# A third buffer for the sums of slots 4 and 12 in the last three groups of a pairwise-bias attention loop, on one Trainium2 core

## The chip, the cores and the metric

The kernel runs on one NeuronCore of a Trainium2 chip. The metric is device time in microseconds, the median of three runs. One further execution was taken by the hardware profiler; durations, waits and the chain of work come from that one.

## The reference, cut to what matters

Two layers work on x of shape 2 x 512 x 32 x 32. Layer 0 is a deformable attention with a learned position bias, followed by an MLP; layer 1 is a plain attention over the 1024 positions. The bias of layer 0 is the part around the change: for each of 16 (batch, head) groups, every one of the 1024 query positions is paired with 64 sampled key positions, and each pair goes through a small network with a hidden width of 128.

```
bias = sign(pos) * log1p(abs(pos))           # pos: 1024 queries x 64 keys x 2
bias = relu(bias @ cpb_w1 + cpb_b1)          # 2 -> 128
bias = relu(bias @ cpb_w2 + cpb_b2)          # 128 -> 128
bias = bias @ cpb_w3 + cpb_b3                # 128 -> 1
sim  = q k^T + bias;  attn = softmax(sim);  out = attn v
x    = x + out_w out + out_b                 # the projection
x    = x + mlp_w2 gelu(mlp_w1 bn(x) + b1) + b2
# layer 1: q, k, v = x W^T + b;  x = x + (softmax(q k^T / sqrt(512)) v) Wp^T + bp
```

## The kernel before

**The loop over slots.** Each of the 16 groups is cut into 16 slots of 4 keys (`NSL = 16`), so the main loop runs over 256 slots, `s = 0..255`. For each slot:

- `st_layer1` (L678) makes the first hidden layer `h` of slot `s + 2` on DVE from two tables `ta` and `tb`. `h` has three buffers.
- `st_layer2` (L695) multiplies `h` by the 128 x 128 weight in four parts z = 0..3 of 32 output channels each. A part is 16 matmuls into one PSUM tile `ps` of 128 x 1024; the pool `zp` has three such tiles. The trace shows every fp32 matmul as two records, so a slot is 64 records. ScalarE (ACT) empties each part with a ReLU: z = 0 and 2 into `rx` (L705), z = 1 into a sums tile, z = 3 into `ub` (both L707).
- `st_sum` (L715) adds z = 0 to z = 1 and z = 2 to z = 3 on DVE.
- An accumulating DMA, issued from POOL (L717), adds `ub` to the slot's sums tile. Further DMAs then fold and join the sums of neighbouring slots: `add` (L734, accumulating, POOL queue) and `move` (L741, plain, SP queue), each chained behind the one before it. The list `due` says at which slot each is issued.
- `st_tables` (L658, L666) makes `ta` and `tb` on ACT for the next four slots once every four slots. It is held behind the eviction of z = 1 of the slot that calls it (`tc.issue_after(evicted[s][0])`).

`st_layer3` (L825) then contracts a whole group's folded sums on the TensorE into `sim`, 22 slots after the group's first slot for the last three groups and 27 slots after it for the others. Softmax (`softmax_steps`) runs in small pieces inside later slots; its transposes on the TensorE are `pt` (L842) and `pb` (L877), and `sim` starts with the product of L806.

**Sums tiles.** Which sums tile a slot's z = 1 part goes to depends on `s % 8`:

```
name, bufs = (
    ("rx", 3), (("u8", 4), ("uo", 3), ("uc", 2), ("uo", 3), ("u4", 2), ("uo", 3), ("uc", 2), ("uo", 3))[s % 8],
    ("rx", 3), ("ub", 3),
)[z]
o = lp.tile([P, 2, 512], F32, name=name, bufs=bufs)
```

In the trace `u8` and `u4` both appear as `u`. Slots with `s % 8 == 4` are the group's slots 4 and 12; they go to `u4`, which has two buffers. For groups before the last three (`s < FULL = 208`) slot 4's sums are joined into slot 0's by the last level of DMAs, and `st_layer3` reads two tiles of a group. In the last three groups this level is left out, and `st_layer3` reads four: those of slots 0, 4, 8 and 12 (in the last group the tiles of its last four slots singly, in place of that of slot 12 alone). So a `u4` tile then lives until its group's `st_layer3`.

**What sets the order.** A scheduler orders each engine's instructions when the program is built, from the program's order, from hints such as `issue_after` and from when buffers come free. At run time each engine works through its own list in order.

**Behind the loop.** The projection of batch 0 is a Strassen-like product of 7 parts (`project`, L1024). It needs sums of its operands beside the operands: `op_blocks` lays them out, `spread` (L125, L128) makes sums of `qa`, `fold` (L119) sums of `vp`. For batch 0, three sums of `qa` are in `op0x` and one overwrites a block of `qa`; the eight operations are put on DVE one at a time in the loop, four slots apart, from the slot `ready` on at which the preparation of the last keys ends. These tiles are in the pool `op`, which is opened at that slot. The order of the parts is 1, 2, 5, 6, 7, 3, 4; the sum number 3 of `spread`, `x[6]`, is read by the last of them alone.

The MLP follows in 8 units (two batches, four parts). `layer1` of a unit makes three interleaved pairs of products in `twice` (L160, with evictions at L166, L170, L172 and L176), writes them to seven blocks `hm[:, 0..6]`, applies GELU (L1096) and makes the sums for `layer2` (L1077), for which blocks 4, 5 and 6 are overwritten at the end. In the first unit the remaining product of `c11` is made first (`first`, L1136 to L1137), copied to `r3`, which is `hm[:, 5]`, added to `c11` at step 13.5 and followed by the GELU at step 19.5. Step 14 starts the third pair of products, whose results go to `hm[:, 4]` and `hm[:, 5]`.

Of the kernel before, what the change touches and what calls it, by code (L numbers as in the profile page):

```python
# [8 lines left out]
F32 = mybir.dt.float32  # L9
# [5 lines left out]
P = 128  # L15
# [42 lines left out]
def conv_seq_kernel(ctx: ExitStack, tc: tile.TileContext, x, xt, kst, pst, cst, vec, wsm, outw, w1, w2, wl, wlt, brow, out):  # L58
    nc = tc.nc
# [56 lines left out]
    def fold(engine, w, sign=ALU.add, which=range(4)):  # L116
        for i in which:
            o, u, v = FOLD[i]
            engine.tensor_tensor(w[o], w[u], w[v], ALU.add if i % 2 else sign)  # L119

    def spread(x, which=range(4)):
        for i in which:
            if i % 2 == 0:
                o, u = ((4, 0), (1, 3))[i // 2]
                nc.vector.tensor_tensor(x[o], x[u], x[1], ALU.subtract)  # L125
            else:
                o, u, v = ((5, 4, 3), (6, 5, 2))[i // 2]
                nc.vector.scalar_tensor_tensor(x[o], x[u], -1.0, x[v], ALU.mult, ALU.subtract)  # L128
# [7 lines left out]
    def plus(out, a, b_, op=ALU.add):  # L136
        nc.vector.tensor_tensor(out, a, b_, op)  # L137
# [53 lines left out]
    def op_blocks(b, parts, wsum):  # L191
        v, q = vp[:, b * NCH : b * NCH + NCH, :], qa[:, b]
        w = [v[:, k : k + 2, n : n + 256] for k, n in ((0, 0), (2, 0), (2, 256), (0, 256))]
        x = [q[:, k : k + 2, n : n + 512] for k in (0, 2) for n in (0, 512)]
        return w + [wsum[:, j] for j in range(3)], x + [parts[:, j] for j in range(3)]

    zp = ctx.enter_context(tc.tile_pool(name="zp", bufs=3, space=PSUM))
    simpp = tc.tile_pool(name="simp", bufs=2, space=PSUM)
# [8 lines left out]
    with tc.tile_pool(name="lp", bufs=2) as lp:  # L207
# [350 lines left out]
        def later():  # L558

            for c in range(NCH):  # L560
                ps = flat("psu")
                for f_, h_, f, h in QUADS:
                    nc.tensor.matmul(
                        ps[h_, f * 512 : f * 512 + 256], wv[f_, c * P + 64 * f : c * P + 64 * f + 64],
                        ow_s[f_, c, h * 256 : (h + 1) * 256], start=True, stop=True,
                    )
                for f_, h_, f, h in QUADS:
                    nc.scalar.copy(uo[f_, c, h * 256 : (h + 1) * 256], ps[h_, f * 512 : f * 512 + 256])
                if c % 2 == 1:
                    yield  # L570
            yield from sample(0)
            for ci in range(1, len(CHAINS)):
                yield from chain(ci)
                yield from sample(ci)
# [113 lines left out]
        def st_layer2(s):  # L688
            h1 = h1s.pop(s)
            r = []  # L690
            for z in range(4):
                ps = zp.tile([P, 2, 512], F32, name="ps2")
                for h in range(2):
                    for q in range(4):
                        nc.tensor.matmul(  # L695
                            ps[32 * q : 32 * q + 32, h, :], cw2[:, 32 * z : 32 * z + 32],
                            h1[:, 16 * h : 16 * h + 16, q, :], start=True, stop=True,
                        )
                name, bufs = (
                    ("rx", 3), (("u8", 4), ("uo", 3), ("uc", 2), ("uo", 3), ("u4", 2), ("uo", 3), ("uc", 2), ("uo", 3))[s % 8],  # L700
                    ("rx", 3), ("ub", 3),
                )[z]
                o = lp.tile([P, 2, 512], F32, name=name, bufs=bufs)
                if z % 2 == 0:
                    nc.scalar.activation(o, ps, AF.Relu, bias=sc[:, 4 + z : 5 + z])  # L705
                else:
                    nc.scalar.activation(o, ps, AF.Relu, bias=sc[:, 4 + z : 5 + z], scale=sc[:, z : z + 1])  # L707
                r.append(o)
                if z % 2 == 1:
                    evicted.setdefault(s, []).append(nc.cur_bb.bb.instructions[-1])  # L710
            sums[s] = r
# [69 lines left out]
        FULL = NS - 3 * NSL  # L781
# [103 lines left out]
        bg = later()  # L885
# [4 lines left out]
        for s in range(NS):  # L890
            if s > 0:
                st_sum(s - 1, 2)
            for _, go, a in sorted(due.get(s, ()), key=lambda e: e[0]):
                go(a)
            if s % 4 == 0 and s // 4 + 1 < 4 * NG:
                load_tables(s // 4 + 1)
            if s + 2 < NS:
                st_layer1(s + 2)
            st_layer2(s)


            if s % 4 == 0 and s // 4 + 1 < 4 * NG:
                with tc.issue_after(evicted[s][0]):
                    st_tables(s // 4 + 1)
            st_sum(s, 0)

            if bg is not None and (s % 4 or s < 124):
                with tc.issue_after(evicted[s][1]):
                    next(bg, None)
            if bg is not None and state.get(len(CHAINS) - 1, 0) is None:  # L910

                bg = None
                php.__exit__(None, None, None)
                opp = tc.tile_pool(name="op", bufs=1, side="right")
                op = opp.__enter__()
                op0 = op_blocks(
                    0, op.tile([P, 3, 2, 512], F32, name="op0x"), op.tile([P, 3, 2, 256], F32, name="op0w")
                )
                ready = s
            if bg is None and s > ready and (s - ready) % 4 == 0 and (s - ready) // 4 <= 8:  # L920
                i = (s - ready) // 4 - 1
                if i < 4:
                    spread(op0[1], (i,))
                else:
                    fold(nc.vector, op0[0], which=(i - 4,))

            if tails and (s % (2 if s < 60 else 4) or s >= NS - NSL):
                with tc.issue_after(evicted[s][s % 4 == 0]):
                    if next(tails[0], 0) is not None:
                        tails.pop(0)  # L930
            for t in (27, 22):
                if s % NSL == t % NSL and s >= t and (s - t < FULL) == (t == 27):
                    st_layer3(s - t)
                    tails.append(softmax_steps((s - t) // NSL))
# [4 lines left out]
                pass  # L939
        tail = softmax_steps(NG - 1)  # L940
        next(tail)


    def load_g(g, i):
# [27 lines left out]
    with ExitStack() as top, tc.tile_pool(name="wp", bufs=1) as wp:  # L972
# [120 lines left out]
        def layer1(p, we, w, xb, xe, hm, others=(), early=False):  # L1093
            def gelu(blk, src, scale=1.0):
                for m in range(2):
                    nc.scalar.activation(  # L1096
                        hm[:, blk, m, :], src[:, m, :], AF.Gelu,
                        bias=col("mb1", 4 * p + 2 * (blk // 2) + m), scale=scale,
                    )

            c11, c12, c21, c22, r5, r3 = (hm[:, j] for j in range(6))

            def weights(q, j):
                a = FIRST_W[PARTS[q][0]]
                return [inner_w(w, we, a, a - 1)[j]]

            def moving(q, j):
                b_ = FIRST_X[PARTS[q][1]]
                return [inner_x(xb, xe, b_, b_ - 1)[j]]

            def dest(g, m, h):
                return hm[:, 2 * g : 2 * g + 2, m, 256 * h : 256 * h + 256]

            def done(g):
                if g == 0:
                    plus(c12, c12, c11)
                elif g == 1:
                    plus(c22, c22, c12)
                    plus(c21, c21, c22)
                    gelu(2, c21, -1.0)  # L1120
                else:
                    plus(c22, c22, r5)
                    gelu(3, c22, -1.0)
                    plus(c12, c12, r5)
                    plus(c12, c12, r3)
                    gelu(1, c12)

            def second():
                ps = mq.tile([P, 2, 512], F32, tag="ps2", name="sw")
                product(w, xb)(ps, 0, 0)  # L1130
                plus(c11, c11, ps)
                gelu(0, c11)

            def first():
                ps = mq.tile([P, 2, 512], F32, tag="ps2", name="sw")
                product(w, xb)(ps, 0, 0)  # L1136
                nc.scalar.copy(r3, ps)  # L1137

            plain = ((21, second),)
            if early:  # L1140
                plain = (-1, first), (13.5, lambda: plus(c11, c11, r3)), (19.5, lambda: gelu(0, c11))
            twice(mq, ((1, 6), (4, 7), (5, 3)), weights, moving, dest, done, (*plain, *others))
            spread([hm[:, j] for j in range(7)])

# [52 lines left out]
        for i, (b, p) in enumerate(units):  # L1197

            j, k = divmod(i, NCH)
# [8 lines left out]
            hm = cp.tile([P, 7, 2, 512], F32, tag="big", name="hm")  # L1208
# [388 lines left out]
```

## Time and profile before

| | |
|---|---|
| median of 3 runs | 2617.9 us (2617.56 to 2618.49) |
| the profiled execution | 2619.14 us, its span 2617.3 us |
| PE busy | 2599.8 us (99% of the span) |
| DVE busy | 2301.5 us (88%) |
| ACT busy | 1752.4 us (67%) |
| POOL busy | 980.2 us (37%) |
| L695, second layer | 16384 records, 1773.3 us |
| L678, first layer on DVE | 257 instructions, 1131.6 us, 4404 ns each |

The span is the time from the first to the last instruction of the profiled execution. The busy time of PE is that of its matmuls, which overlap and whose ends are modelled; short waits of PE can hide in it. "Idle before" in a row is the idle time of the engine ahead of an instruction, with what ended it. The granted TensorE clock was 0.999 in the profiled execution.

### The profile page before, as it was taken

How to read it: one execution, taken by the hardware profiler on the slowest of the kernel's cores; microseconds unless marked ns; L12 is line 12 of the kernel's file. 1: busy time of each engine (PE TensorE's matmuls, PEld its weight loads, DVE VectorE, ACT ScalarE, POOL GpSimd, SP SyncE). 2: the span in 40 equal slices, each digit the busy share in tenths (PEclk: the TensorE clock that was granted, in tenths of full speed). 3: DMA queues.
4: the chain of work that ended last, by engine and by line, in shares of the span. 5: the costliest groups of instructions: out<-in, count | busy, mean ns of one | idle time of the engine just before them, and what ended most of it. 6: DMA issues, size and time to landing. Idle time of an engine off the chain costs nothing.

```text
span 2617.3 us, 48989 instructions
## 1 busy us (share of the span) xinstructions
PE 2599.8 (99%) x19660; PEld 1011.9 (39%) x19660; DVE 2301.5 (88%) x1459; ACT 1752.4 (67%) x2362; POOL 980.2 (37%) x1122
## 2 busy tenths in 40 slices
PE   9999999999999999999999999999999999999999
PEld 3332333333233233323333332332355655646556
DVE  6999999999999999999999999998776587666656
ACT  5887888888888988888788777777733242314041
POOL 1344444445444444444444444333332334200100
PEclk9999999999999999999999999999999999999999
DMA  5889999899989999899999899778777768400202
GB/s 186 174 191 193 199 195 194 191 194 190 203 187 190 188 205 198 181 191 203 190 198 192 183 193 194 169 167 182 156 202 170 149 146 169 90 16 1 73 1 56
DMA packets 177634, 428.27 MB, mean 164 GB/s; under 512 B 30048, under 2 KB 78320, under 8 KB 174720
## 3 DMA queue, kind: packets, MB, share of 16 engines
q0 software_dynamic: 107392, 273.09, 58.3%
q1 hardware_dynamic: 69584, 151.75, 17.4%
q8 instruction: 155, 2.54, 0.4%
q14 instruction: 71, 0.58, 0.1%
q10 hardware_dynamic: 432, 0.31, 0.0%
HBM read 82.16 MB, written 6.55 MB: 34 GB/s over the span
## 4 chain that ended last, share of the span: by engine, by line
PE 92%; DVE 4%; issue 2%; ACT 1%; DMA 1%; POOL 0%; DVEq 0%; ACTq 0%; POOLq 0%
PE ps L695 64%; PE sw L1077 7%; PE sw L1246 7%; PE sw L160 6%; PE sw L1024 2%; PE sw L1344 2%; PE psg L597 1%; DVE hm L137 1%; PE sim L825 1%; PE psx L1322 1%; DVE h L678 0%; DMA uc<-uc 0%; ACT rx L705 0%; PE sim L806 0%; PE pt L842 0%
## 5 line engine op out<-in xcount | busy, mean ns | idle before, releaser
L695 PE MATMUL ps<-h,cw 128*32 128x512 f32 x16384 | 1773.3, 592 | 5.2 <-ACT rx L705 3.3
L678 DVE CUSTOM_DVE_ANT_1 h<-ta,tb 128x4096 f32<-128x4096 f32 (+1 forms) x257 | 1131.6, 4404 | 25.9 <-PE ps L695 21.5
L695 PEld LDWEIGHTS ps<-h,cw 128*32 128x32 f32 x16384 | 529.7, 110 | 1216.8 <-issue 1144.1
L705 ACT ACTIVATE rx<-ps,sc 128x1024 f32<-128x1024 f32 x512 | 568.2, 1110 | 149.5 <-PE ps L695 111.5
L734 POOL DMA_DIRECT2D u<-u x397 | 409.0, 1507 | 15.1 <-DMA u<-ub 12.6
L707 ACT ACTIVATE ub<-ps,sc 128x1024 f32<-128x1024 f32 x256 | 308.3, 1204 | 87.0 <-PE ps L695 86.6
L715 DVE SCALAR_TENSOR_TENSOR ub<-rx,sc,ub 128x1024 f32<-128x1024 f32 x256 | 327.9, 1281 | 10.7 <-ACT ub L707 10.7
L717 POOL DMA_DIRECT2D uo<-ub x127 | 112.5, 886 | 589.1 <-DVE ub L715 552.0
L1077 PE MATMUL sw<-hm,w2t 128*128 128x512 f32 x448 | 194.3, 593 | 0.3 <-DVE hm L125 0.2
L707 ACT ACTIVATE uo<-ps,sc 128x1024 f32<-128x1024 f32 x128 | 154.1, 1204 | 40.0 <-PE ps L695 38.1
L715 DVE SCALAR_TENSOR_TENSOR uo<-rx,sc,uo 128x1024 f32<-128x1024 f32 x128 | 164.0, 1281 | 3.4 <-ACT uo L707 2.8
L734 POOL DMA_DIRECT2D u<-uc x126 | 126.7, 1264 | 19.1 <-DMA u<-uc 17.3
L717 POOL DMA_DIRECT2D uc<-ub x64 | 55.5, 867 | 188.1 <-DVE ub L715 154.7
L1077 PEld LDWEIGHTS sw<-hm,w2t 128*128 128x128 f32 x448 | 84.9, 190 | 104.2 <-issue 97.7
L717 POOL DMA_DIRECT2D u<-ub x64 | 54.9, 857 | 182.1 <-DVE ub L715 179.0
L137 DVE TENSOR_TENSOR hm<-hm,sw 128x512 f32<-128x512 f32 x79 | 57.6, 732 | 74.1 <-PE sw L160 51.1
L734 POOL DMA_DIRECT2D uc<-uc x63 | 106.3, 1687 | 2.3 <-DMA uc<-ub 2.3
L734 POOL DMA_DIRECT2D uc<-uo x63 | 102.8, 1632 | 10.8 <-DMA uc<-uo 10.4
L1410 POOL DMA_DIRECT2D xs<-rs x6 | 7.2, 1200 | 259.1 <-DVE rs L137 259.1
L707 ACT ACTIVATE u<-ps,sc 128x1024 f32<-128x1024 f32 x64 | 77.1, 1204 | 24.5 <-PE ps L695 20.8
L658 ACT ACTIVATE ta<-fb,vs 128x512 f32<-128x512 f32 (+1 forms) x65 | 89.0, 1373 | 5.8 <-DMA fb<-fdr 5.8
L707 ACT ACTIVATE uc<-ps,sc 128x1024 f32<-128x1024 f32 x64 | 77.0, 1203 | 21.6 <-PE ps L695 18.4
(297 smaller groups left out, 2644.9 us busy)
## 6 DMA issues: line engine op xcount, KB each, us to landing
uo<-ub POOLq DMA_DIRECT2D x127, 512.0 KB, 5.4
fb<-fdr SPq DMA_DIRECT2D x64, 512.0 KB, 5.8
u<-ub POOLq DMA_DIRECT2D x64, 512.0 KB, 6.5
uc<-ub POOLq DMA_DIRECT2D x64, 512.0 KB, 6.1
u<-u POOLq DMA_DIRECT2D x63, 256.0 KB, 7.0
u<-uo SPq DMA_DIRECT2D x63, 256.0 KB, 5.8
u<-uo POOLq DMA_DIRECT2D x63, 256.0 KB, 7.3
uc<-uc POOLq DMA_DIRECT2D x63, 256.0 KB, 8.1
```

The lines of the kernel that those rows point to most:

```text
L137: nc.vector.tensor_tensor(out, a, b_, op)
L160: nc.tensor.matmul(bank[:, e, :], w, x, start=(q in (1, 2, 5) and e == k == 0), stop=True, skip_group_check=True,)
L658: nc.scalar.activation(ta.rearrange("p j x -> p x j")[:, :, j0:j1], fb[:, 0, :, j0:j1], AF.Identity, bias=col("cb1"), scale=col("w1x"),)
L678: nc.vector._custom_dve(TENSOR_ADD_SAT, out=h1[:, y : y + step].rearrange("p y t x -> p (y t x)"), in0=a.unsqueeze(1).to_broadcast([P, ste ...
L695: nc.tensor.matmul(ps[32 * q : 32 * q + 32, h, :], cw2[:, 32 * z : 32 * z + 32], h1[:, 16 * h : 16 * h + 16, q, :], start=True, stop=True,)
L705: nc.scalar.activation(o, ps, AF.Relu, bias=sc[:, 4 + z : 5 + z])
L707: nc.scalar.activation(o, ps, AF.Relu, bias=sc[:, 4 + z : 5 + z], scale=sc[:, z : z + 1])
L715: nc.vector.scalar_tensor_tensor(r[1], r[0], sc[:, z : z + 1], r[1], ALU.mult, ALU.add)
L717: nc.gpsimd.dma_start(out=sums[s][1], in_=sums[s][3], accum_op=ALU.add)
L734: nc.gpsimd.dma_start(out=out, in_=in_, accum_op=ALU.add)
L1077: nc.tensor.matmul(ps[:, m, :], w[:, a, k, m * P : (m + 1) * P], x[:, b_, k, :], start=(k == 0), stop=(k == 1),)
L1246: nc.tensor.matmul(ps[:, m, :], w[:, a, k, c + m * P : c + (m + 1) * P], x[b_][:, k, :], start=(k == 0), stop=(k == nk - 1),)
```

## The change

- The z = 1 part of slots with `s % 8 == 4` takes, in the last three groups, a third tile `x6` in the pool `op` in every third turn. These six slots are 212, 220, 228, 236, 244 and 252; `x6` is for 228 and 252, and the two buffers of `u4` are for the other four.
- `op0x` has two blocks instead of three. The fourth sum of `qa`, `x[6]`, is allocated as the next `x6` tile behind the loop and made there (`spread(op0[1], (3,))`), no longer in the loop. The operations that stay in the loop are seven, so the folds of `vp` come four slots earlier.
- In the first MLP unit the first product is copied to `hm[:, 6]` instead of `hm[:, 5]`, and its addition to `c11` and the GELU stand together at step 21.

```diff
-        return w + [wsum[:, j] for j in range(3)], x + [parts[:, j] for j in range(3)]
+        return w + [wsum[:, j] for j in range(3)], x + [parts[:, j] for j in range(parts.shape[1])]
...
-                o = lp.tile([P, 2, 512], F32, name=name, bufs=bufs)
+                pool = lp
+                if z == 1 and s % 8 == 4 and s >= FULL and (s - FULL) // 8 % 3 == 2:
+                    pool, name, bufs = op, "x6", 1
+                o = pool.tile([P, 2, 512], F32, name=name, bufs=bufs)
...
-                    0, op.tile([P, 3, 2, 512], F32, name="op0x"), op.tile([P, 3, 2, 256], F32, name="op0w")
+                    0, op.tile([P, 2, 2, 512], F32, name="op0x"), op.tile([P, 3, 2, 256], F32, name="op0w")
...
-            if bg is None and s > ready and (s - ready) % 4 == 0 and (s - ready) // 4 <= 8:
+            if bg is None and s > ready and (s - ready) % 4 == 0 and (s - ready) // 4 <= 7:
                 i = (s - ready) // 4 - 1
-                if i < 4:
+                if i < 3:
                     spread(op0[1], (i,))
                 else:
-                    fold(nc.vector, op0[0], which=(i - 4,))
+                    fold(nc.vector, op0[0], which=(i - 3,))
...
         tail = softmax_steps(NG - 1)
         next(tail)
+        op0[1].append(op.tile([P, 2, 512], F32, name="x6", bufs=1))
+        spread(op0[1], (3,))
...
-                nc.scalar.copy(r3, ps)
+                nc.scalar.copy(hm[:, 6], ps)
 
-            plain = ((21, second),)
-            if early:
-                plain = (-1, first), (13.5, lambda: plus(c11, c11, r3)), (19.5, lambda: gelu(0, c11))
+            def merge():
+                plus(c11, c11, hm[:, 6])
+                gelu(0, c11)
+
+            plain = ((-1, first), (21, merge)) if early else ((21, second),)
```

## The prediction

> **What bounds the kernel now.** I read the page first: PE is busy 99% of the span, and the chain of waits gives it 92%. So only idle time of PE, and what keeps it idle, is worth anything. The groups' mean can't show that, since 256 slots are averaged; I went to the table by stage, cut at the transposes `pb`, which bound stretches of known work:
>
> ```profile
> 1455.27:1680.49 225.22, 225.22 (x2090) 68.58 (x2090) 222.92 (x106) 170.98 (x197) 101.93 (x121) 1.00 0.91 191
> 1680.49:1849.87 169.38, 166.09 (x1529) 52.35 (x1530) 152.42 (x72) 125.44 (x157) 58.33 (x68) 1.00 0.80 171
> 1849.87:1891.63 41.76, 40.97 (x359) 12.48 (x359) 32.16 (x19) 30.17 (x48) 14.68 (x17) 1.00 0.74 150
> ```
>
> Columns: length, then busy time (instructions) of PE, PEld, DVE, ACT, POOL, then granted clock, DMA share, GB/s. In the first stretch PE has no idle time: 32 slots and 5.07 us of other matmuls (pb 1.02, pt 0.58 and 0.59, sim 0.86, 1.02 and 1.00 by the chain) make (225.22 - 5.07) / 32 = 6.88 us a slot. The second has 23 slots (1472 records of L695) and 6.89 us of others (1.02, 1.79, 0.59, 0.59, 1.02, 1.88): 23 x 6.88 + 6.89 = 165.1. It took 169.38, so **4.25 us are lost**. The timeline of PE says where most of it is:
>
> ```profile
> 1711.92 20.81 PE L695 MATMUL ps<-h,cw 128*32 128x512 f32 x192 [0.21 <-DVE h L678]
> ...
> 1806.02 3.64 PE L695 MATMUL ps<-h,cw 128*32 128x512 f32 x32 [0.41 <-ACT rx L705]
> 1811.56 7.07 PE L695 MATMUL ps<-h,cw 128*32 128x512 f32 x64 [1.89 <-ACT rx L705]
> ...
> 1829.07 20.81 PE L695 MATMUL ps<-h,cw 128*32 128x512 f32 x192 [0.69 <-DVE h L678]
> ```
>
> Four waits, 3.20 us; the rest is pipeline refill after each and a slow stretch at 1694.8. They come in two clusters, and ACT shows their common cause:
>
> ```profile
> 1704.31 1.20 ACT L707 ACTIVATE u<-ps,sc 128x1024 f32<-128x1024 f32 x1 [0.50 <-PE sim L825]
> ...
> 1821.56 1.20 ACT L707 ACTIVATE u<-ps,sc 128x1024 f32<-128x1024 f32 x1 [1.65 <-PE sim L825]
> ```
>
> An eviction that should follow its own matmuls (L695) follows L825 of another group. These are z = 1 of slots 228 and 244, each the third `u4` tile of the last three groups: it waits until `st_layer3` of the group before has read the first. The part's matmuls were done at about 1685.2 and 1798.8 (evictions of the neighbouring parts), so the PSUM tile was held for some 19 and 23 us. Meanwhile PE ran on two PSUM tiles, the tables tied to this eviction came late, `h` with them.
>
> The loop's end has one more wait, in the chain:
>
> ```profile
> 1886.23 0.70 issue
> 1886.92 2.77 PE sim L825 x12
> 1889.69 0.09 issue
> ```
>
> and POOL says of what:
>
> ```profile
> 1861.79 0.81 POOL L734 DMA_DIRECT2D u<-uc  x1 [6.22 <-DMA u<-uc]
> ...
> 1884.28 0.82 POOL L734 DMA_DIRECT2D u<-uc  x1 [5.00 <-DMA u<-uc]
> ```
>
> The last L734 landed at 1886.83. Followed back, one DMA waits for the landing of another, or stands behind it on POOL, through 1884.28, 1876.68, 1867.60, 1862.30, 1852.10, 1839.33 and 1831.62 to `u<-ub` at 1824.37: slot 244's own, late by the held eviction.
>
> **What the Trainium skill says.** "Perfetto Trace Analysis", Optimization Strategy: a gap that repeats on the engine that should be saturated can mean that SBUF or PSUM had no room for the next tile. The trace agrees, two clusters at the same slot of the buffer's turn. "PSUM — Partial Sum Buffer", Engine vs sequencer instructions: ACT, DVE and POOL work strictly first in, first out; so a waiting instruction holds all behind it, which the POOL rows show. "DMA: Bandwidth & Descriptors", Two DMAs through the same engine are not ordered: a dependent DMA has to wait for the first one's completion semaphore; here the 5.00 us ahead of 1884.28.
>
> **The change, part by part.**
>
> *Buffers.* No instruction is added, two evictions get another target. Slot 228 takes the unused `x6`. Slots 236 and 244 take the tiles of 212 and 220, which L825 had read by 1704.3, 40 us or more before. Slot 252 takes `x6` again, read at about 1821.5 and needed at about 1865. Nothing waits, and the changed program's order confirms it: on ACT the eviction stands between its neighbours of z = 0 and z = 2, the tables next; DVE and PE order are regular. Gain: the excess, **4.25**. Low end 3.2 (listed waits alone); high 4.5.
>
> *Loop end.* Slot 244's `u<-ub` then goes out some 20 us earlier against its slot. The last waits need only 0.70 and 0.09: **0.8**. Ends 0 (the chain finds another anchor) and 1.0 (refill too). What would be late next is the last `ub` sum, below.
>
> *The moved sum.* One L128, 1.22 us on DVE, leaves the loop at 1457.1. The chain from 1303.7 to 1688.6 is all PE, so DVE's time there is covered: 0, no gain. It returns on DVE ahead of the last L715, and must wait for L825 to have read `x6`. With the wait of 0.70 gone: L825 from 1886.2, `x6` read at 1886.2 + 2 x 0.86 + 0.2 = 1888.15 (0.86 for each four records, the first four being slot 248's); L128 to 1889.4; `ub` sum to 1890.75. PE comes to `sim<-ub` after 5.7 us of queued matmuls, at 1891.9. Covered by 1.15 us: **0**, bounded by 0 and -1.3 (its price if the cover is gone). Its reader is the last part of the projection, 23 us on. No DMA is moved; POOL and SP keep theirs, some a place earlier.
>
> *First MLP unit.*
>
> ```profile
> 1959.64 0.58 ACT L166 COPY hm<-sw 128x512 f32<-128x512 f32 x1
> ...
> 1960.28 1.99 PE L160 MATMUL sw<-xe,w1e 128*128 128x256 f32 x8 [1.16 <-ACT hm L166]
> ```
>
> L166 writes `hm[:, 4:6]` and had to wait for the addition that read `r3` (DVE, until 1959.45). With `hm[:, 6]` it waits for PE alone and can run at 1957.4: 1.16 us gone. But the table load (1.28 us, idle-free before the GELU) stays ahead of the next copy on ACT: L176 to 1959.75, load to 1961.0, GELU, L170 to 1962.25, where PE could go on at 1961.5: 0.8 lost. And PE's order has one L1077 less between the last two L160 pairs, so it waits for L176 another 0.8. That is -0.4; the L1077 isn't lost, but done later in a list without waits, and by 1967.5 both programs stand level, so 0 by this count. Ends -0.6 and +1.16; I take their middle, **+0.3**.
>
> Sum: 4.25 + 0.8 + 0 + 0.3 = 5.35. Against the profiled execution, 2619.14 - 5.35 = 2613.8; the median of the runs is 1.2 below that execution, so 2617.9 - 5.35 = **2612.5**.
>
> **The rivals.**
>
> *Only the two stalls go.* The DMA chain at the end has another anchor: its share of DMA time is high, and after 1862 each link is about 5 us whatever began it. Against it: `uc<-ub` of 1862.30 had its sum at about 1855.7, so it stood 6.6 us in the queue. Gain 4.25: 2613.6.
>
> *The first unit's wait goes whole.* If the scheduled order hides L170 and L176 better than I count: 4.25 + 0.8 + 1.16 = 6.2: 2611.7.
>
> *The change doesn't do what it says.* The held PSUM tile costs little by itself (0.4 us in the first cluster), and the loss would be due to the DMA and table work of that place. Then it stays: about 2617.6. Against it: ACT's releaser is L825 both times, nothing else.
>
> *Slower: the wait moves to slot 252.* `x6` has one buffer. If its release by group 14 came after slot 252's eviction, that would be held as slot 244's was, 23 us; `u<-ub` of slot 252, at 1873.91 with 4.8 us to land, has 9 us until L825 reads it, so 14 us would reach the end, with 0.4 for the first cluster and 0.3 for the unit gained, and the chain's 3.5 lost later instead of sooner: 2617.9 + 13 = 2631. It decides only from a release over 40 us late (1821.5 to 1865); nothing points there.
>
> **How the numbers follow.** A measurement of this kernel can tell about 0.2%, 5.2 us, from no change: the bound is 2612.7. Forecast (5.35, itself uncertain by 0.8): 0.62, of it 0.44 beyond the bound and 0.18 within. First unit whole: 0.20, faster. Only the stalls: 0.10, and no effect: 0.04, both within. Slot 252: 0.04, slower. So faster 0.64, same 0.32, slower 0.04. The range, 2610.9 to 2614.6, takes in gains of 3.3 (low ends) to 7.0 (all high ends) and leaves out the last two cases and the edges.
>
> **What would show it.** The stretch between the same two `pb` should take about 165 us, with no `u` or `x` eviction released by L825. PE should pass from L695 to the last L825 without an issue gap, and POOL's last waits for DMA be shorter than 5 us. `sim<-ub` must not wait for DVE. In the first unit, L160 should wait twice for ACT by under 1 us. It is wrong if the stretch stays over 167, if POOL's chain still ends after the last L695, or if the last L715 comes after PE is ready for it.

## The result, and the profile after

| | before | after |
|---|---|---|
| median of 12 runs each | 2618.41 us | 2613.04 us |
| ratio after / before | | 0.9976, 95% interval 0.9967 to 0.9985 |
| the profiled execution and its span | 2619.14, 2617.3 us | 2612.25, 2610.5 us |

The change makes the kernel faster by 5.4 us by the medians and by 6.3 us (3.9 to 8.6) by the ratio. Two of the twelve runs of before took 2623.7 and 2624.3 us and the other ten at most 2619.1, while no run of after took more than 2614.2: the ratio takes these two in, the medians hardly do. The forecast was 2612.5 us. In this section and below, lines behind the edits have moved: L695 is still L695, but L705, L707, L715, L717, L734, L741 and L825 are now L708, L710, L718, L720, L737, L744 and L828, and L806, L1024, L1077 and L1096 are L809, L1029, L1082 and L1101. The traces of before and of the two experiments built on it, b_unit and i_lag_b, keep the old numbers.

The table by stage of after, cut at the same two `pb`, then at the projection's first product, and last the first MLP unit up to the next unit's first L160 (columns as in the prediction):

```profile
1680.02:1845.15 165.13, 165.13 (x1532) 50.37 (x1529) 158.02 (x73) 126.16 (x157) 60.15 (x72) 1.00 0.83 177
1845.15:1885.66 40.51, 40.51 (x363) 12.76 (x359) 29.14 (x19) 30.35 (x48) 12.92 (x16) 1.00 0.72 147
1936.33:1983.18 46.85, 46.51 (x149) 27.54 (x148) 27.14 (x32) 18.59 (x26) 16.29 (x14) 1.00 0.82 190
```

PE has no idle time left in the first two stages. Cut at the first record of the same instructions, before has 169.38, 41.83 and 47.48 us, so the gains are 4.25, 1.32 and 0.63: 6.20 in sum. (The prediction's mark at the second `pb` stood 0.07 us late, hence its 41.76.) The two spans differ by 6.86 us; the rest lies where nothing was meant to change, 0.40 ahead of 1455 and 0.26 behind the unit. Differences of that size there mean nothing: over all the traces below, the stretch ahead of that first `pb` takes 1454.7 to 1456.0 us and the one behind the unit 625.9 to 628.0.

ACT's timeline shows that slot 228's eviction now follows its own matmuls, with the tables next:

```profile
1684.75 1.21 ACT L710 ACTIVATE x<-ps,sc 128x1024 f32<-128x1024 f32 x1 [0.60 <-PE ps L695]
1685.86 1.37 ACT L658 ACTIVATE ta<-fb,vs 128x512 f32<-128x512 f32 x1
```

PE's timeline at the loop's end: the last L695 starts at 1867.50 and runs into L828 without an idle entry, and `sim<-ub` follows the first product of the projection:

```profile
1867.50 13.94 PE L695 MATMUL ps<-h,cw 128*32 128x512 f32 x128
1881.26 1.04 PE L828 MATMUL sim<-u,w3f 128*32 128x512 f32 x4
...
1885.66 1.13 PE L1029 MATMUL sw<-qa,vp 128*128 128x512 f32 x2
1886.71 0.62 PE L828 MATMUL sim<-ub,w3u 128*32 128x512 f32 x1
```

### The profile page after: what moved, and what is told of

Read it like the earlier page. It is cut to its first block, busy times and chain, and to the rows that moved or that the text cites. A ratio compares the mean times of both kernels' runs of the same rounds, so it can differ in the third digit from the quotient of the medians.

```text
span 2610.5 us, 49004 instructions
## 1 busy us (share of the span) xinstructions
PE 2597.5 (100%) x19660; PEld 1009.8 (39%) x19660; DVE 2303.7 (88%) x1459; ACT 1754.3 (67%) x2362; POOL 980.6 (38%) x1122
## 4 chain that ended last, share of the span: by engine, by line
PE 96%; DVE 3%; ACT 1%; issue 0%; DMA 0%; DVEq 0%; ACTq 0%
PE ps L695 67%; PE sw L1082 7%; PE sw L1253 7%; PE sw L160 7%; PE sw L1029 2%; PE sw L1351 2%; PE psg L597 1%; PE sim L828 1%; DVE hm L137 1%; PE psx L1329 1%; PE sim L809 0%; PE pt L845 0%; PE pkv L534 0%; PE pb L880 0%; PE psq L333 0%
## 5 line engine op out<-in xcount | busy, mean ns | idle before, releaser
L695 PE MATMUL ps<-h,cw 128*32 128x512 f32 x16384 | 1772.0, 592 | 1.8 <-ACT rx L708 1.0
L695 PEld LDWEIGHTS ps<-h,cw 128*32 128x32 f32 x16384 | 527.7, 110 | 1214.0 <-issue 1160.4
L708 ACT ACTIVATE rx<-ps,sc 128x1024 f32<-128x1024 f32 x512 | 568.6, 1111 | 138.4 <-PE ps L695 115.5
L737 POOL DMA_DIRECT2D u<-u x394 | 406.9, 1514 | 2.5 <-issue 2.2
L710 ACT ACTIVATE ub<-ps,sc 128x1024 f32<-128x1024 f32 x256 | 308.4, 1205 | 90.6 <-PE ps L695 90.5
L720 POOL DMA_DIRECT2D uo<-ub x127 | 111.4, 877 | 600.1 <-DVE ub L718 570.0
L718 DVE SCALAR_TENSOR_TENSOR ub<-rx,sc,ub 128x1024 f32<-128x1024 f32 x256 | 327.3, 1278 | 3.1 <-ACT ub L710 3.1
L1082 PE MATMUL sw<-hm,w2t 128*128 128x512 f32 x448 | 194.0, 592 | 0.2 <-DVE hm L125 0.2
L710 ACT ACTIVATE uo<-ps,sc 128x1024 f32<-128x1024 f32 x128 | 154.3, 1205 | 43.9 <-PE ps L695 40.7
L718 DVE SCALAR_TENSOR_TENSOR uo<-rx,sc,uo 128x1024 f32<-128x1024 f32 x128 | 163.7, 1279 | 7.6 <-ACT uo L710 7.0
L737 POOL DMA_DIRECT2D u<-uc x124 | 124.8, 1280 | 17.6 <-DMA u<-uc 15.3
L1082 PEld LDWEIGHTS sw<-hm,w2t 128*128 128x128 f32 x448 | 84.9, 190 | 104.0 <-issue 97.9
L720 POOL DMA_DIRECT2D uc<-ub x64 | 55.4, 866 | 179.9 <-DVE ub L718 147.9
L137 DVE TENSOR_TENSOR hm<-hm,sw 128x512 f32<-128x512 f32 x79 | 57.6, 732 | 73.0 <-PE sw L160 50.6
L720 POOL DMA_DIRECT2D u<-ub x62 | 53.1, 856 | 178.8 <-DVE ub L718 178.8
L737 POOL DMA_DIRECT2D uc<-uc x63 | 107.6, 1708 | 0.0
L737 POOL DMA_DIRECT2D uc<-uo x63 | 102.8, 1632 | 10.6 <-DMA uc<-uo 10.3
L737 POOL DMA_DIRECT2D u<-uo x62 | 84.8, 1368 | 21.6 <-DMA u<-uo 18.4
L710 ACT ACTIVATE uc<-ps,sc 128x1024 f32<-128x1024 f32 x64 | 77.0, 1203 | 21.2 <-PE ps L695 19.3
```

Source lines behind the costliest of these rows:

```text
L695: nc.tensor.matmul(ps[32 * q : 32 * q + 32, h, :], cw2[:, 32 * z : 32 * z + 32], h1[:, 16 * h : 16 * h + 16, q, :], start=True, stop=True,)
L718: nc.vector.scalar_tensor_tensor(r[1], r[0], sc[:, z : z + 1], r[1], ALU.mult, ALU.add)
L720: nc.gpsimd.dma_start(out=sums[s][1], in_=sums[s][3], accum_op=ALU.add)
L737: nc.gpsimd.dma_start(out=out, in_=in_, accum_op=ALU.add)
L1082: nc.tensor.matmul(ps[:, m, :], w[:, a, k, m * P : (m + 1) * P], x[:, b_, k, :], start=(k == 0), stop=(k == 1),)
```

## The experiments

One table holds what the traces of all kernels show; the stages are those above (loop: `pb` to `pb`; end: `pb` to projection; unit), in us, each from one profiled execution. The ratio is to runs of the kernel before on the same chip; the medians of before there were 2618.4 to 2618.9 us.

| kernel | what differs | loop | end | unit | median | ratio, 95% interval |
|---|---|---|---|---|---|---|
| before | | 169.38 | 41.83 | 47.48 | 2618.4 | |
| after | the change | 165.13 | 40.51 | 46.85 | 2613.0 | 0.9976 (0.9967 to 0.9985) |
| a_loop | after, unit undone | 165.13 | 40.51 | 47.48 | 2612.4 | 0.9974 (0.9964 to 0.9984) |
| b_unit | before, unit alone | 169.46 | 42.02 | 46.85 | 2617.7 | 0.9994 (0.9986 to 1.0003) |
| d_244 | a_loop, only 228 held | 165.68 | 44.87 | 47.48 | 2619.6 | 0.9999 (0.9991 to 1.0007) |
| e_228 | a_loop, only 244 held | 166.42 | 41.68 | 47.48 | 2616.7 | 0.9991 (0.9983 to 0.9999) |
| i_lag_d | d_244, less work on DVE | 165.68 | 40.51 | 47.48 | 2613.5 | 0.9973 (0.9964 to 0.9982) |
| i_lag_b | before, less work on DVE | 166.90 | 41.79 | 47.48 | 2616.6 | 0.9992 (0.9984 to 1.0001) |
| g_rx | a_loop, tile for z = 0 | 167.94 | 46.04 | 47.47 | 2616.8 | 0.9996 (0.9988 to 1.0005) |
| g_rx2 | the same, another execution | 167.94 | 41.59 | 47.48 | 2616.6 | one run |
| f_table | after, early table load | 165.13 | 40.51 | 46.43 | 2612.2 | 0.9974 (0.9963 to 0.9984) |

**a_loop and b_unit: do the parts add up?** a_loop keeps the buffers and the moved sum and leaves the unit as it was (the diff is against after); b_unit has the unit's new lines alone, on the kernel before.

```diff
-                nc.scalar.copy(hm[:, 6], ps)
...
-            plain = ((-1, first), (21, merge)) if early else ((21, second),)
+                nc.scalar.copy(r3, ps)
...
+                plain = (-1, first), (13.5, lambda: plus(c11, c11, r3)), (19.5, lambda: gelu(0, c11))
```

> The third buffer and the moved sum, with the first MLP unit left as it was. Theory (three separate gains add up): the pb-to-pb stretch takes 165.1 us, the stretch from that pb to the first product of the projection 40.5, the first unit 47.6 as before; together 5.5 us faster than before, and about 0.8 slower than with the whole change. Rival (the unit gains only because the loop's end changed what ACT or DVE still have to do there): the unit takes 46.9 here too, and the whole gain of 6.3 us is there.

> The edit of the first MLP unit alone, on the kernel before. Theory: the loop and its end stay at 169.4 and 41.8 us, and the unit takes 46.85 us instead of 47.64, 0.8 us faster in all. The prediction's own count of this edit was +0.3 (from -0.6 to +1.16), so a gain of 0.3 would say that the loop's end helped the unit, and 1.16 that the table load hides wholly here.

They add up to the hundredth in the stages: the unit's 0.63 us are there without the loop's part and missing without the unit's. The loop and the end of b_unit, where nothing differs from before, are 0.08 and 0.19 us longer, so two traces of one piece of program can differ by that much. In the whole time 0.6 us can't be seen. The stretch behind the unit, the same program in all of them, takes 625.9 us in a_loop, 626.8 in b_unit, 627.3 in after and 627.6 in before.

**d_244 and e_228: one held eviction each.** Both are a_loop with another condition for the extra tile `x6`.

```diff
-                if z == 1 and s % 8 == 4 and s >= FULL and (s - FULL) // 8 % 3 == 2:
+                if z == 1 and s == 244:             # d_244: slot 228 is held, 244 isn't
+                if z == 1 and s in (228, 244):      # e_228: 244 waits for 228's tile
```

> Only slot 244 takes the extra tile; slot 228 waits for its group's predecessor as before; the unit is left as it was. Theory (the loop's end was late because of slot 244's sums): the first cluster of waits stays, some 0.5 us, so the pb-to-pb stretch takes 165.6 to 165.8 us, and the end takes 40.5; 4.9 us faster than before. Rival (the end has its own anchor, the bandwidth of the last DMAs or the moved sum): the stretch is the same, but the end stays at 41.8, and the gain is 3.7 us.

> Only slot 228 gets the extra tile of its own; slot 244 takes the same tile next and waits for it until the st_layer3 of the group before, as it did; the unit is left as it was. Theory: only the first cluster goes, so the pb-to-pb stretch takes 168.8 us (0.5 us less), the second cluster and the end stay (41.8); 0.5 us faster than before, which is no measurable change. Rival (the first delay is carried on through the DMA queue and makes the second dear): the second cluster shrinks with the first, and the stretch takes 167 us or less.

Both of my expectations were wrong in one half. In d_244 the loop is as expected, but the end is later than in before, which has both holds (44.87 against 41.83), and nothing is gained in all. In e_228 the loop gains 2.96 us instead of 0.5, and falls below the rival's bound of 167: the second cluster, 3.7 us in before (169.38 less 165.68), costs only 1.3 when slot 228 was not held. (The profiled execution of e_228, 2614.3 us, lies 2.4 below its median; behind the unit alone it is 1.3 us shorter than before, so only its stages are compared here.) So the first hold, which costs PE 0.55 us on the spot (165.68 against 165.13), costs it much more later. Stages of d_244, then of e_228:

```profile
1680.32:1846.00 165.68, 165.47 (x1532) 51.44 (x1528) 156.50 (x73) 125.29 (x157) 58.45 (x69) 1.00 0.82 174
1846.00:1890.87 44.87, 42.40 (x363) 13.21 (x359) 28.00 (x18) 30.33 (x48) 14.63 (x17) 0.96 0.69 142
```

```profile
1679.98:1846.40 166.42, 165.55 (x1532) 51.46 (x1528) 153.32 (x72) 126.03 (x157) 58.32 (x69) 1.00 0.81 174
1846.40:1888.08 41.68, 41.12 (x363) 12.52 (x359) 32.33 (x19) 30.17 (x48) 14.63 (x17) 1.00 0.74 150
```

**Where the debt is kept: DVE.** For each slot I took, from the traces, the end of its `ub` sum (L718), counted from the slot's first L695 (a slot is 64 records, two for each of 32 matmuls; a part is thus 8 matmuls, not 16 as said at the start):

| slot | 233 | 237 | 240 | 243 | 246 | 248 |
|---|---|---|---|---|---|---|
| after | 12.74 | 12.80 | 12.74 | 12.74 | 12.74 | 12.74 |
| before | 13.17 | 17.40 | 16.98 | 16.50 | 9.67 | 13.31 |
| d_244 | 13.17 | 17.40 | 16.98 | 16.49 | 16.18 | 13.03 |
| e_228 | 12.74 | 12.80 | 12.74 | 12.74 | 9.67 | 13.31 |

With slot 228 held, the tables are late: 1705.41 in before, 1685.86 in after. DVE gets one `h` behind, and makes two in a row when it has them. DVE's timeline of before:

```profile
1707.35 8.76 DVE L678 CUSTOM_DVE_ANT_1 h<-ta,tb 128x4096 f32<-128x4096 f32 x2 [0.52 <-ACT tb L666]
```

DVE's timeline around slot 237, first d_244, then after:

```profile
1753.07 4.42 DVE L678 CUSTOM_DVE_ANT_1 h<-ta,tb 128x4096 f32<-128x4096 f32 x1
1757.40 1.28 DVE L718 SCALAR_TENSOR_TENSOR uo<-rx,sc,uo 128x1024 f32<-128x1024 f32 x1
1758.60 4.42 DVE L678 CUSTOM_DVE_ANT_1 h<-ta,tb 128x4096 f32<-128x4096 f32 x1
1762.94 1.28 DVE L718 SCALAR_TENSOR_TENSOR ub<-rx,sc,ub 128x1024 f32<-128x1024 f32 x1
```

```profile
1753.21 4.42 DVE L678 CUSTOM_DVE_ANT_1 h<-ta,tb 128x4096 f32<-128x4096 f32 x1
1757.55 1.28 DVE L718 SCALAR_TENSOR_TENSOR ub<-rx,sc,ub 128x1024 f32<-128x1024 f32 x1
1758.74 1.28 DVE L718 SCALAR_TENSOR_TENSOR uc<-rx,sc,uc 128x1024 f32<-128x1024 f32 x1
1760.01 4.42 DVE L678 CUSTOM_DVE_ANT_1 h<-ta,tb 128x4096 f32<-128x4096 f32 x1
```

The `ub` sum of slot 237 is that at 1762.94 in d_244 and that at 1757.55 in after: in d_244 an `h` (start to start 4.34 us) still stands ahead of it. Up to slot 236 DVE's list, in the programs that hold slot 228, puts the sums ahead of the `h`; that hides the missing `h` from the sums, and PE works from the three `h` buffers. From 237 on the two lists have the same order, and the sums are 4.6 us late. A slot of DVE work takes 4.34 + 2 x 1.2 = 6.73 us (1753.07 less 1746.34, the `h` before) of PE's 6.87, so it regains 0.14 us a slot, as the row of d_244 shows up to slot 243. Most of the debt is repaid at once in slot 246, which takes PE 9.74 us because 2.87 us of L809 and L828 stand in it: 16.18 falls to 13.17 in slot 247. From slot 237 to 244 nothing of these 4.6 us shows in PE, whose slots take 6.87 us in d_244 as in after (one of them 6.94 in d_244).

In before, the second hold comes before the debt is repaid. ACT's first wait of the second cluster, in before:

```profile
1810.39 1.11 ACT L705 ACTIVATE rx<-ps,sc 128x1024 f32<-128x1024 f32 x1 [3.32 <-DVE ub L715]
```

ACT waits for an `rx` tile until a late sum has read it; PE's 1.89 us is that wait. In d_244 nothing stops PE there, and POOL passes the lateness to the end. POOL's timeline of d_244, then of after:

```profile
1821.07 0.84 POOL L737 DMA_DIRECT2D uc<-uo  x1 [8.11 <-DMA uc<-uo]
...
1831.08 0.81 POOL L737 DMA_DIRECT2D u<-uc  x1 [6.55 <-DMA u<-uc]
...
1848.22 0.84 POOL L737 DMA_DIRECT2D uc<-uo  x1 [8.01 <-DMA uc<-uo]
...
1882.11 0.82 POOL L737 DMA_DIRECT2D u<-uc  x1 [4.88 <-DMA u<-uc]
```

```profile
1830.60 0.88 POOL L720 DMA_DIRECT2D uo<-ub  x1 [3.22 <-DVE ub L718]
...
1837.47 0.88 POOL L720 DMA_DIRECT2D u<-ub  x1 [3.42 <-DVE ub L718]
...
1844.34 0.88 POOL L720 DMA_DIRECT2D uo<-ub  x1 [3.94 <-DVE ub L718]
```

In after, POOL waits for sums: it is ahead of its work. In d_244 its long waits from 1821 on are for DMAs; one chain behind another, it does not catch up in 60 us, though DVE is within 0.3 us of its time again by slot 248.

**i_lag_d and i_lag_b: is the debt the cause?** Four sums, 4.8 us of DVE, are left out just after the lag has come out; the z = 0 part of slots 238 to 241 is then missing from the result. In the traces ACT, POOL and SP have the same instructions in the same order as in d_244 (for i_lag_b, as in before), and DVE has all but these four. So the order that the scheduler chose, which does differ between d_244 and after, is no rival here.

```diff
-            st_sum(s, 0)
+            st_sum(s, 0) if not 238 <= s <= 241 else None
```

> The kernel with the extra tile for slot 244 only (d_244), and the first sum of slots 238 to 241 left out on DVE (their z = 0 part is lost from the result): four times 1.2 us of DVE time, 4.8 in all, no other instruction changes place. Theory (the first held eviction leaves DVE late, the ub sums ending 17.4 us after their slot's first matmul instead of 12.7, and that lag reaches the end through the DMA queue): the ub sums are at 12.7 again from slot 242, the pb-to-pb stretch takes 165.7 us as in d_244, and the end falls from 44.9 to 40.5, 4.9 us faster than the kernel before. Rival (the end of d_244 is late for the DMAs' own sake: slot 252's tile, or bandwidth): the end stays at 44.9.

> The kernel before, with the first sum of slots 238 to 241 left out on DVE (their z = 0 part is lost from the result); both evictions are held as before. Theory (the second hold is dear because DVE comes to it 4 us late): the second cluster falls from 3.6 to some 1.3 us, as in e_228, and the pb-to-pb stretch takes about 167.0 instead of 169.4; the end stays at 41.7. Rival (a hold at slot 244 costs what it costs, and e_228 gained by its first hold and its tiles alone): 169.4.

Both came out as the theory said, so the debt on DVE is shown to be what makes the end of d_244 late and most of what the second cluster costs in before. In i_lag_d the `ub` sums are at 13.39 in slot 240 and 12.74 from 241 on, the end is 40.51 to the hundredth of after, and the kernel is as fast as after, though slot 228 is still held: none of its nine runs took more than 2614.5 us, and none of the thirteen of d_244 less than 2617.1. POOL's timeline of i_lag_d:

```profile
1831.93 0.88 POOL L720 DMA_DIRECT2D uo<-ub  x1 [2.92 <-DVE ub L718]
...
1838.80 0.88 POOL L720 DMA_DIRECT2D u<-ub  x1 [3.43 <-DVE ub L718]
```

In i_lag_b the second cluster falls as expected (166.90 for about 167.0), and ACT's wait for `rx` of 3.32 us is down to 1.08:

```profile
1807.95 1.11 ACT L705 ACTIVATE rx<-ps,sc 128x1024 f32<-128x1024 f32 x1 [1.08 <-DVE ub L715]
```

The end stays at 41.79 with slot 244 held, in e_228 as well (41.68). So slot 244's own hold makes the end 1.2 to 1.3 us late.

**g_rx: the other half of what a hold ties up.** The extra tile goes to z = 0, so that the held sum takes no `rx`.

```diff
-                if z == 1 and s % 8 == 4 and s >= FULL and (s - FULL) // 8 % 3 == 2:
+                if z == 0 and s in (228, 244):
```

> The extra tile goes to the other half of the held sum: z = 0 of slots 228 and 244 takes it in place of an rx tile, while z = 1 still waits for st_layer3 of the group before; the unit is left as it was. Theory (a held eviction ties up an rx tile beside the PSUM tile, and PE's 1.9 us wait came through ACT waiting for rx): ACT no longer waits 3.3 us for DVE there, the second cluster falls from 3.6 to about 1.3 us, and the pb-to-pb stretch takes about 167.0. Rival (the PSUM tile and DVE's lag alone make it dear): 169.4. The end, which hangs on slot 244's sums and on DVE's lag, stays at 41.7 or comes later.

> The same program as g_rx, one more look: of its twelve runs nine took 2615.6 to 2618.2 us and three 2621.9 to 2622.9, and the profile was of one of the three. Theory (the three had one DMA link more at the loop's end): in a run of the first kind the pb-to-pb stretch takes 167.0 to 168.0 us as there, and the end 41.7 instead of 46.0. Rival (the end is 46.0 in all of them): then the time is made up elsewhere.

Only partly so. ACT does not wait for `rx` there any more, but DVE is as late as before (the `ub` sum of slot 243 at 16.50), and ACT next waits for a `uc` tile that a DMA still reads. ACT in g_rx2:

```profile
1813.40 1.20 ACT L710 ACTIVATE uc<-ps,sc 128x1024 f32<-128x1024 f32 x1 [1.69 <-DMA u<-uc]
```

The loop takes 167.94 us: 1.44 gained of 2.4. The two profiled executions of this one program took 2621.9 and 2616.6 us, and their traces tell where they differ: 46.04 against 41.59 us in the end. So an end of this kind is one draw and no mean. Of before one trace is kept; whether its end varies as much is not shown.

**f_table: the rest of the unit's waits.**

```diff
             def first():
+                nc.scalar.activation(hm[:, 5, 0, 0:1], col("mb1", 0), AF.Gelu)
```

> The kernel after, with one GELU of a single column in front of the first MLP unit (its result is overwritten later and not read), so that the activation table is loaded while ACT is idle. Theory (the 0.8 us that PE still waits in the unit is the 1.28 us load in front of L170): the unit takes 46.1 us instead of 46.85, and the whole is 0.7 us faster than after. Rival (PE waits there for DVE's additions and the order of the list, or a load comes back in front of the unit's own GELU): 46.6 or more, no difference.

The load now lies in idle time of ACT (L1140 is the GELU that was put in), and the unit gains 0.42 us, between the two theories. It is the shortest of all in the stages, but its whole time can't be told from that of after. ACT, then PE, in f_table:

```profile
1933.96 1.28 ACT L1140 ACT_TABLE_LOAD   x1 [14.00 <-PE sw L1029]
```

```profile
1953.79 2.28 PE L160 MATMUL sw<-xe,w1e 128*128 128x256 f32 x8
1955.91 1.03 PE L160 MATMUL sw<-xb,w1e 128*128 128x256 f32 x4
```

## Why the prediction was right, and where it was not

**Loop buffers, 4.25 us: right to the hundredth,** because it was counted as the whole excess of the stage, not wait by wait. The explanation beside it was incomplete. It gave each hold its own cluster, and said that PE ran on two PSUM tiles meanwhile. e_228 and i_lag_b show that of the 3.7 us of the second cluster only 1.2 to 1.3 belong to slot 244's hold; the rest is the debt of slot 228's, kept by DVE for ten slots, 237 to 246. Relieving slot 244 alone gave nothing that can be measured (ratio 0.9999, 0.9991 to 1.0007; 0.7 us in loop and end), slot 228 alone about half (3.1 of 5.6 us in loop and end; ratio 0.9991, 0.9983 to 0.9999, where both give 0.9974).

**Loop end, 0.8 us (0 to 1.0): mis-sized, 1.32 was measured.** The listed idle of 0.70 and 0.09 leaves out what overlapping records hide: from start to start, PE lost 0.88 and 0.29 us there beyond its usual pace. The end of the range should have been higher. Slot 244's `u<-ub` as the anchor is supported by e_228 and i_lag_b. But it is not the only possible one: d_244, without that hold, ends later still. The rival "another anchor" put it among the last DMAs; in d_244 it lay on DVE, ten to twenty slots ahead.

**Moved sum, 0: right, by the predicted cover.** L128 ran at the place predicted, and the `ub` sum behind it ended at 1884.34 + 1.28 = 1885.62; PE came to `sim<-ub` at 1886.71: 1.1 us, predicted 1.15. DVE in after:

```profile
1883.19 1.22 DVE L128 SCALAR_TENSOR_TENSOR x<-op0x,qa 128x1024 f32<-128x1024 f32 x1 [2.48 <-PE sim L828]
1884.34 1.28 DVE L718 SCALAR_TENSOR_TENSOR ub<-rx,sc,ub 128x1024 f32<-128x1024 f32 x1
```

What it costs once the cover is gone was not tried.

**First MLP unit, +0.3 (my own count was 0): mis-sized, 0.63.** ACT and PE in after:

```profile
1953.80 1.28 ACT L1101 ACT_TABLE_LOAD   x1
1955.09 0.72 ACT L1101 ACTIVATE hm<-hm,vs 128x512 f32<-128x512 f32 x1
1955.72 0.56 ACT L170 COPY hm<-sw 128x512 f32<-128x512 f32 x1
```

```profile
1952.98 2.28 PE L160 MATMUL sw<-xe,w1e 128*128 128x256 f32 x8
1955.09 1.03 PE L160 MATMUL sw<-xb,w1e 128*128 128x256 f32 x4
1956.34 1.13 PE L160 MATMUL sw<-xb,w1x 128*128 128x256 f32 x4 [0.21 <-ACT hm L170]
```

The chain on ACT came as counted: L170 ends 19.95 us after the unit's start, to the hundredth of the prediction. PE lost the first 0.8 in two halves, 0.39 inside the eight records at 1952.98 (2.11 to the next start, against 1.72 elsewhere) and 0.39 ahead of 1956.34. The second wait of 0.8, for L176, did not come: L172 runs at 1957.50, L176 at 1959.32, and PE shows 0.1 at most. That step failed. f_table shows that the load is behind half of the first 0.8. The other half stays in f_table, and the traces say of what it is: the fifth of the eight records waits for DVE's L137, which reads a product from PSUM. In after that L137 ends at 1954.07 and the record starts at 1954.13, in f_table at 1954.89 and 1954.94. No run here removes that wait. DVE in after:

```profile
1953.39 0.68 DVE L137 TENSOR_TENSOR hm<-hm,sw 128x512 f32<-128x512 f32 x1
```

**The sum and the signs.** Predicted 5.35, measured 6.20 in the stages, both small terms too low by some 0.5 and 0.3. That the medians differ by 5.4, almost the forecast, is luck: by the ratio it may be anything from 3.9 to 8.6. The range had a slip: its ends, gains of 3.3 and 7.0, are called the low and high ends of all terms, but these add up to 1.3 (3.2 + 0 - 1.3 - 0.6) and 6.7 (4.5 + 1.0 + 0 + 1.16). "First unit whole" (6.2) met the sum by another way: the unit gave 0.63, not 1.16. "Only the stalls" is out, as the end gained; "does nothing" is out; no `u` or `x` eviction of the last groups is released by L828, so slot 252 does not wait. One sign was wrong: POOL's waits at the end are not shorter than 5 us.

```profile
1877.06 0.82 POOL L737 DMA_DIRECT2D u<-uc  x1 [5.47 <-DMA u<-uc]
```

The wait lasts until the transfer ahead of it lands, as it did. What changed is its date: PE's last L695 ends at 1881.44, and this DMA goes out 4.4 us ahead of that; in before it went out at 1884.28, 1.95 us ahead of 1886.23. It lands at 1879.62, 1.8 us before that end, where before it landed 0.6 us after. The very last transfer, `uc<-ub`, still lands 1.0 us after it (1882.44), but 1.4 us before PE reads that `uc` (1883.84). So the length of this wait says nothing, its date does.

## What to carry to other kernels

A late buffer can cost little where it happens and much more 100 us or more later, if the engine behind it has little slack in each turn (here DVE, 0.14 us in 6.87). To find it, compare when its results come, counted from the start of their turn, between a slot far from the stall and one just behind it. Two stalls of one cause need not be additive (here 3.1 and 0.7 us alone, 5.6 together); relieving only one may give nothing, so count the whole stage's excess and relieve both. Read waits from start to start, since overlapping records hide some tenths of each (here 0.88 us lost where 0.70 is listed).

## What the runs showed of the hardware that I had not expected

The 2.65 us that PE lost from start to start ahead of L828 in d_244 make only part of the 4.36 us by which its end is longer. The rest goes with the clock. Stage and PE of d_244:

```profile
1884.70:1887.70 3.00, 2.94 (x8) 0.91 (x10) 0.45 (x1) 0.09 (x1) 0.00 (x0) 0.58 0.81 153
```

```profile
1884.76 1.56 PE L828 MATMUL sim<-u,w3f 128*32 128x512 f32 x4 [2.47 <-issue]
1886.04 1.98 PE L828 MATMUL sim<-u,w3u 128*32 128x512 f32 x4
```

PE stood idle for 2.47 us, and soon after it began again, at 1885.17, the granted clock fell to 0.50 for 3.4 us; 0.58 is the mean of the stretch shown, which begins a little earlier. A record of L828 then took up to 1061 ns instead of 592, and the products from the first L828 to the projection 6.11 us instead of 4.40: 1.7 us more. It came in g_rx too, 0.50 from 1888.65 to 1892.07, after 3.50 us of idle time, and in no kernel after the waits of up to 1.9 us. The Trainium skill, "TensorE: Matmul & The Clock Gate", HAM oscillation — how this bites in real kernels, speaks of gaps over about 3.4 us; here 2.47 were enough. So in these traces a wait of PE at the loop's end has a price that jumps: the one of 0.70 us cost 0.88, the one of 2.47 us cost 4.36. Where between 1.9 and 2.47 us of idle time the jump begins was not tried.
